# Layer 0's scan: one product moved from GpSimd to Vector, edges read in place, norm weight and bias fused, a new pace for the planner

## The chip, the cores and the metric

The kernel runs on one core of a Trainium2 chip. A core has TensorE (PE, with weight loads PEld), VectorE (DVE), ScalarE (ACT), GpSimd (POOL) and SyncE (SP), each with its own queue of instructions that it works off in order, and 16 DMA engines. The metric is device time in microseconds. Engines wait for each other through semaphores.

## The reference

The input is x of 4 samples, 96 channels and 128 x 128 pixels. Four layers follow each other, each as x = x + layer(norm(x)). Layer 0 is the one that the change touches; of it, with L = 128 * 128:

```
xz = einsum('oc,bchw->bohw', in_proj_w, x); xc, z = split(xz)
u = silu(depthwise_conv3x3(xc) + conv_b)              # (B, C, L)
xs = stack([u, u reversed])                           # two directions k
dts, Bs, Cs = split(einsum('bkcl,kdc->bkdl', xs, x_proj_w))
delta = softplus(einsum('bkrl,kcr->bkcl', dts, dt_proj_w) + dt_proj_b)
h_l = exp(delta_l * A) * h_(l-1) + delta_l * xs_l * B_l        # the scan over L
y_l = h_l * C_l;  ys = y + D * xs
y = ys[forward] + reversed ys[backward]
y = (y - mean_c) * rsqrt(var_c + 1e-5) * out_norm_w + out_norm_b
out = scale_w * (out_proj_w @ (y * silu(z)))
```

Layer 1 has small convolutions and Fourier transforms of two thirds of the channels. Layer 2 is a deformable convolution: a convolution gives each pixel nine offsets, and at each the four neighbouring pixels are gathered and weighed. Layer 3 transforms the image by a DCT, runs a scan with 16 states over four quadrants, and transforms back.

## The kernel before, in words

Each sample goes through three pieces. The *front* is layer 0, layer 1 and the offsets of layer 2; its results go to DRAM (`x1`, `x2`, `quad_d` with the pixels laid out for gathering, `idx_d`, `w4_d`). The *back* is layer 2's gathering, layer 3's head (`layer3_head`) and its first transform. Then comes layer 3's scan (`layer3`), with nothing beside it.

The main loop puts the back of one sample beside the front of the next one. In time this gives: the front of sample 0 alone (the *head stretch*); three *beside-stretches*, in which a back and a front run together (in the second and third the inverse transform of the sample before also runs beside the front's first block), each followed by layer 3's scan; a last stretch with a back and no front; the last scan and the last inverse.

**Gathering.** One gather (`indirect_dma_start`, tile `l2_g`, shown as `l_g`) is issued by Pool and fetches 128 pixels with four neighbours of 96 channels; there are 128 rows x 9 taps = 1152 gathers a sample. Beside a front there is room for four rows (`rows` = 4 from `back`), so that the gathers of a row wait until the row four before has been weighed. `weigh` multiplies the four neighbours by their weights: for each gather two instructions on Scalar and two on Vector (`l_sm`, `l_part`), and sums over several taps on Vector. PE then transposes and multiplies.

**Layer 0's scan** is the pool `l0b` with its function `scan(k, n)`. Each of the two directions k has 32 chunks of 512 columns, 64 in all, and the generators are staggered so that the directions alternate. For one chunk PE makes `pd`; Scalar makes softplus in three steps (`tmp`, and `dl` by Relu), Vector adds them (`dl + tmp`); PE makes `pB`; Scalar makes `dA = exp(dl * A)`; Vector multiplies `du = uc * pB` and Pool multiplies `du = du * dl`; Vector's `tensor_tensor_scan` makes `h`, starting from the edge of the chunk before in the same direction, which Scalar copies into a tile of its own (`l0_e`); PE makes `pC`, and Vector multiplies `h` by it in place. In the first half of the chunks the product goes to DRAM (`part_d`). In the second half the other direction's product is read back, and a tail follows: PE adds up and centres (`pm`), Scalar squares and copies (`sq`, `ct`), PE makes the variance (`pv`), Scalar makes its inverse root by Ln and Exp, Vector multiplies (`ct * sq`), Scalar applies the norm's weight and bias (Identity), Vector multiplies by `sz`, PE projects (`po`), Vector adds x and takes statistics.

**The order** is made by a planner (`Program`). All instructions of back (lane 0) and front (lane 1) are recorded, not issued. Each lane is first planned alone (`measure`): every instruction gets a start by the costs in `cost` and the times at which its inputs and buffers are ready. These starts become due times: distances between starts are multiplied by the `pace` that was set when the instruction was recorded, and the whole is scaled to 0..1. Then `issue` merges the lanes: among the instructions that can start within 0.17 us of the earliest on that engine, the one with the smallest due time is next. So a lower pace makes a part of the front fall due in less of the back's time. `self.program.pace` is 0.1 over layer 0's scan and 1.0 elsewhere. A DMA's cost is a pair: what the issuing engine is held for, and its landing, for which the model's single DMA resource is held; its data are ready 2.0 us behind that. The merged order is then fixed in each engine's queue. An instruction is issued through a helper, so nearly all of the profile's rows carry line L65 (SP's DMAs L412) and are told apart by their tiles.

Of the kernel before, what the change touches and what calls it, by code (L numbers as in the profile page):

```python
# [22 lines left out]
F32 = mybir.dt.float32  # L23
F32R = mybir.dt.float32r
I32 = mybir.dt.int32
AF = mybir.ActivationFunctionType
ALU = mybir.AluOpType
# [4 lines left out]
C, H, W = 96, 128, 128  # L32
L = H * W
CH = 512
# [202 lines left out]
class Program:  # L237
# [121 lines left out]
    def cost(self, engine, name, out, ins):  # L359

        if engine == "SP":
            v = next(v for v in [out, *ins] if isinstance(v, View) and v.tile.kind == "SBUF")
            return 0.35, 1.4e-5 * v.at[0].size * (v.rows[1] - v.rows[0])
        n = max(out.at[0].size, ins[0].at[0].size if name == "bn_stats" else 0)
        if name == "indirect_dma_start":
            return 1.25, 0.3
        if engine == "PE":
            if name == "transpose":
                return 1.1 * 0.00085 * n, None
            m = out.rows[1] - out.rows[0]  # L370
            share = (0.25 if m <= 32 else 0.5 if m <= 64 else 1.0) if n > 256 else 1.0
            return 1.1 * share * max(0.165, 0.005 + 0.001667 * n), None
        if engine == "ACT":
            return (0.055 + 0.0008 * n if name == "copy" else 0.19 + 0.00079 * n), None
        if engine == "POOL":
            return 0.2 + 0.002 * n, None
        if name == "tensor_tensor_scan":
            return 0.1 + 0.00214 * n, None
        fast = name in ("tensor_copy", "tensor_scalar", "memset") and all(
            v.tile.kind == "SBUF" for v in [out, *ins]  # L380
        )
        late = 0.12 if name == "scalar_tensor_tensor" and n > 200 else 0.0
        return (0.135 if n < 200 else 0.105) + late + n / (1800 if fast else 1024), None
# [128 lines left out]
class Net:  # L512
# [132 lines left out]
    def layer0(self, xin, T, beside):  # L645
        nc, a = self.nc, self.a
        u_d, sz_d, part_d = self.plane("u_d"), self.plane("sz_d"), self.plane("part_d")
        st0, T.st1 = self.stats_tile(), self.stats_tile()
        with self.program.pool(name="l0w", bufs=1) as wp, self.program.pool(name="l0p", bufs=1, space=PSUM) as ps:
# [71 lines left out]
                yield from staggered(jobs + ([beside(ps, wt)] if beside else []), 1)  # L721


            self.program.pace = 0.1
            with self.program.pool(name="l0b", bufs=3) as wb:
                edges = [None, None]

                def scan(k, n):
                    t = n if k == 0 else NCH - 1 - n
                    s = slice(t * CH, (t + 1) * CH)  # L730
                    uc = wb.tile([C, CH], F32, name="l0_uc", tag="uc", bufs=6)
                    nc.sync.dma_start(out=uc, in_=u_d[:, s])
                    second = n >= NCH // 2
                    if second:
                        xc = wb.tile([C, CH], F32, name="l0_x", tag="x", bufs=4)
                        nc.sync.dma_start(out=xc, in_=xin[:, s])
                        sz = wb.tile([C, CH], F32, name="l0_z", tag="z", bufs=4)
                        nc.sync.dma_start(out=sz, in_=sz_d[:, s])
                    yield
                    yield  # L740
                    pd = ps.tile([C, CH], F32, name="l0_pd", tag="b", bufs=1)
                    nc.tensor.matmul(out=pd, lhsT=wd[:, k, :], rhs=uc, start=True, stop=True)
                    yield
                    dl = wb.tile([C, CH], F32, name="l0_dl", tag="dl")
                    tmp = wb.tile([C, CH], F32, name="l0_tmp", tag="tmp")
                    bias = v[:, 1 + k : 2 + k]
                    nc.scalar.activation(tmp, pd, AF.Abs, bias=bias, scale=1.0)
                    nc.scalar.activation(dl, pd, AF.Relu, bias=bias, scale=1.0)
                    nc.scalar.activation(tmp, tmp, AF.Exp, scale=-1.0)
                    nc.scalar.activation(tmp, tmp, AF.Ln, bias=1.0, scale=1.0)  # L750
                    nc.vector.tensor_tensor(dl, dl, tmp, ALU.add)
                    pB = ps.tile([C, CH], F32, name="l0_pB", tag="c", bufs=2)
                    nc.tensor.matmul(out=pB, lhsT=wbc[:, 2 * k, :], rhs=uc, start=True, stop=True)
                    yield
                    dA = wb.tile([C, CH], F32, name="l0_dA", tag="dA")
                    nc.scalar.activation(dA, dl, AF.Exp, scale=negA[:, k : k + 1])
                    du = wb.tile([C, CH], F32, name="l0_du", tag="du")
                    nc.vector.tensor_tensor(du, uc, pB, ALU.mult)
                    yield
                    nc.gpsimd.tensor_tensor(du, du, dl, ALU.mult)  # L760
                    yield
                    h = wb.tile([C, CH], F32, name="l0_h", tag="h", bufs=5)
                    prev = edges[k]
                    if k == 0:
                        nc.vector.tensor_tensor_scan(
                            h, dA, du, 0.0 if prev is None else prev, ALU.mult, ALU.add
                        )
                        edge = h[:, CH - 1 : CH]
                    else:
                        nc.vector.tensor_tensor_scan(  # L770
                            h[:, ::-1], dA[:, ::-1], du[:, ::-1],
                            0.0 if prev is None else prev, ALU.mult, ALU.add,
                        )
                        edge = h[:, 0:1]
                    edges[k] = wb.tile([C, 1], F32, name="l0_e", tag="edge", bufs=6)
                    nc.scalar.copy(edges[k], edge)
                    if second:
                        part = self.load(wb, part_d[:, s], [C, CH], "l0_part", 3)
                    pC = ps.tile([C, CH], F32, name="l0_pC", tag="c", bufs=2)
                    nc.tensor.matmul(out=pC, lhsT=wbc[:, 2 * k + 1, :], rhs=uc, start=True, stop=True)  # L780
                    yield
                    nc.vector.tensor_tensor(h, h, pC, ALU.mult)
                    if not second:
                        nc.sync.dma_start(out=part_d[:, s], in_=h)
                        yield
                        return
                    yield


                    pm = ps.tile([C, CH], F32, name="l0_pm", tag="a", bufs=2)  # L790
                    nc.tensor.matmul(out=pm, lhsT=center[:, 1, :], rhs=uc, start=True, stop=False)
                    nc.tensor.matmul(out=pm, lhsT=center[:, 0, :], rhs=part, start=False, stop=False)
                    nc.tensor.matmul(out=pm, lhsT=center[:, 0, :], rhs=h, start=False, stop=True)
                    yield
                    ct = wb.tile([C, CH], F32, name="l0_ct", tag="ct")
                    sq = wb.tile([C, CH], F32, name="cn_s", tag="sq")
                    nc.scalar.activation(sq, pm, AF.Square)
                    nc.scalar.copy(ct, pm)
                    yield
                    pv = ps.tile([C, CH], F32, name="cn_v", tag="a", bufs=2)  # L800
                    nc.tensor.matmul(out=pv, lhsT=self.cavg, rhs=sq, start=True, stop=True)
                    yield
                    nc.scalar.activation(sq, pv, AF.Ln, bias=self.eps[:C], scale=1.0)
                    nc.scalar.activation(sq, sq, AF.Exp, scale=-0.5)
                    yield
                    nc.vector.tensor_tensor(ct, ct, sq, ALU.mult)
                    yield
                    nc.scalar.activation(ct, ct, AF.Identity, bias=v[:, 8:9], scale=v[:, 7:8])
                    yield
                    nc.vector.tensor_tensor(ct, ct, sz, ALU.mult)  # L810
                    yield
                    po = ps.tile([C, CH], F32, name="l0_po", tag="a", bufs=2)
                    nc.tensor.matmul(out=po, lhsT=woT, rhs=ct, start=True, stop=True)
                    yield
                    nc.vector.scalar_tensor_tensor(xc, po, v[:, 9:10], xc, ALU.mult, ALU.add)
                    nc.vector.bn_stats(T.st1[:, t, :], xc)
                    nc.sync.dma_start(out=T.x1[:, s], in_=xc)
                    yield

                yield from staggered((scan(k, n) for n in range(NCH) for k in range(2)), 2)  # L820

    def layer1(self, T):
# [1562 lines left out]
```

## Time and profile before

| what | us |
|---|---|
| time before, median of 3 (15122.8 to 15134.95) | 15123.15 |
| the profiled execution's own time | 15123.18 |
| its span | 15121.3 |
| PE, DVE, ACT, POOL busy | 12434.4, 11294.8, 8958.7, 10394.8 |

Where the stretches lie, by the first and last start of their instructions in the trace (us from the span's start):

| stretch | layer 0's scan (`pd` first, last) | gathers first, last | transform's last copy (`l_xo`) |
|---|---|---|---|
| head | 263.8, 590.9 | none | none |
| beside 1 | 1727.5, 2149.6 | 1304.1, 3163.9 | 3375.9 |
| beside 2 | 5354.6, 5764.3 | 4836.4, 6720.4 | 6933.9 |
| beside 3 | 8913.8, 9325.3 | 8397.4, 10277.7 | 10488.5 |
| last (no front) | none | 11949.5, 13413.1 | 13591.4 |

The scan's end lies some 30 to 40 us behind its last `pd`. In the second beside-stretch the front's pieces start at: statistics 4848, convolution 4943, scan 5355, layer 1's transforms 5876 (their last product 6211), layer 1's convolution 6248, offsets 6551 (last 6906).

How to read the profile: a group's row gives the line, engine, operation, output and input tiles, forms and count; then busy us and the mean ns of one; then the idle time just before them and what ended it. A row of windows gives, for each engine, busy us and in brackets the number of instructions, then the clock that PE was granted, the DMA engines' share and GB/s. Each fp32 product of PE appears as two records, so 128 records of `pd` are 64 products.

### The profile page before, as it was taken

What the parts mean: (1) busy time and instruction counts of PE and PEld (TensorE: products, weight loads), DVE (VectorE), ACT (ScalarE), POOL (GpSimd) and SP (SyncE); (2) the same over time, 40 slices, a digit from 0 to 9 for tenths busy, and PEclk for the clock granted to TensorE, in tenths of its full rate; (3) what the DMA queues carried; (4) which work ended last, traced back from release to release, by engine and by line L of the source; (5) the groups of instructions that cost most, each with busy time, mean ns of one, the idle gap of its engine ahead of it and who ended that gap; (6) DMA issues with size and microseconds to landing.
All of it is one profiled execution on the core that took longest, in us unless ns stands there. A gap on an engine that the chain in (4) does not pass through costs nothing. (4 is left out here: it accounts for less than half of the span.)

```text
span 15121.3 us, 175326 instructions
## 1 busy us (share of the span) xinstructions
PE 12434.4 (82%) x48096; PEld 5808.6 (38%) x48096; DVE 11294.8 (75%) x21519; ACT 8958.7 (59%) x21605; POOL 10394.8 (69%) x7936
## 2 busy tenths in 40 slices
PE   7897887879997978888999688888999744459998
PEld 3353334343332334444333233534333422233334
DVE  3626686668998587677999578666999765548997
ACT  3614685556664576555666467555666465546664
POOL 2104747748998765765999674773999877748997
PEclk9997898989998989989999899998999855579999
DMA  4546659766666767876666765976666755556666
GB/s 115 143 127 201 191 167 253 229 201 183 187 197 193 234 181 213 239 218 185 194 189 194 218 208 167 259 227 192 194 188 194 216 171 165 167 149 181 189 197 192
DMA packets 1326732, 2914.81 MB, mean 193 GB/s; under 512 B 282864, under 2 KB 768944, under 8 KB 1211440
## 3 DMA queue, kind: packets, MB, share of 16 engines
q1 hardware_dynamic: 1027376, 1997.21, 45.8%
q0 software_dynamic: 298368, 906.38, 20.2%
q8 instruction: 382, 6.26, 0.2%
q14 instruction: 606, 4.96, 0.1%
HBM read 2455.28 MB, written 447.48 MB: 192 GB/s over the span
## 5 line engine op out<-in xcount | busy, mean ns | idle before, releaser
L65 POOL DMA_INDIRECT l_g<-quad_d,l_i x4608 | 4648.1, 1009 | 2541.0 <-issue 1319.5
L65 POOL TENSOR_TENSOR l_hc<-l_h,l_cl 128x1024 f32<-128x1024 f32 x1536 | 3609.7, 2362 | 287.9 <-DVE l_h L65 259.0
L65 PE MATMUL l_py<-l_hc,ident 128*128 128x512 f32 x6144 | 3068.4, 610 | 185.9 <-POOL l_hc L65 182.4
L65 DVE TENSOR_TENSOR_SCAN l_h<-l_dA,l_carry,l_dB 128x512 f32<-128x512 f32 x2304 | 2863.6, 1266 | 1.7
L65 DVE SCALAR_TENSOR_TENSOR l_sm<-l_g,l_v,l_sm 128x96 f32<-128x96 f32 x4608 | 1491.3, 324 | 1137.8 <-ACT l_sm L65 1041.2
L65 ACT ACTIVATE l_dA<-l_dl,l_al 128x512 f32<-128x512 f32 x2304 | 1637.4, 718 | 1111.6 <-DVE l_h L65 1102.3
L65 ACT ACTIVATE l_sm<-l_g,l_v 128x96 f32<-128x96 f32 x4608 | 1677.6, 369 | 731.2 <-DMA l_g<-quad_d,l_i 634.4
L65 ACT ACTIVATE l_part<-l_g,l_v 128x96 f32<-128x96 f32 x4608 | 1654.8, 363 | 234.9 <-DVE l_sm L65 234.4
L65 PEld LDWEIGHTS l_py<-l_hc,ident 128*128 128x128 f32 x6144 | 1133.6, 192 | 1352.9 <-issue 829.2
L65 PE MATMUL l_pc<-l_sT,l_wk 128*96 128x256 f32 (+1 forms) x3584 | 1244.2, 471 | 418.8 <-ACT l_sT L65 418.1
L65 PE MATMUL l_pt<-ident,l_sm 128*128 128x128 f32 (+1 forms) x3584 | 798.3, 327 | 909.4 <-DVE l_sm L65 827.9
L65 DVE TENSOR_TENSOR l_dB<-l_du,l_pB 128x512 f32<-128x512 f32 x2304 | 1493.9, 678 | 49.5 <-POOL l_du L65 26.7
L65 DVE SCALAR_TENSOR_TENSOR l_part<-l_g,l_v,l_part 128x96 f32<-128x96 f32 x4608 | 1485.8, 323 | 36.3 <-ACT l_part L65 35.6
L65 PE MATMUL l_pB<-l_bc,pick 128*128 128x512 f32 x2304 | 1399.8, 635 | 135.4 <-DVE l_dB L65 121.5
L65 POOL TENSOR_TENSOR l_dP<-l_du,l_cl 128x512 f32<-128x512 f32 x768 | 978.6, 1274 | 101.0 <-DMA l_cl<-bc_d 74.6
L65 PEld LDWEIGHTS l_pt<-ident,l_sm 128*128 128x128 f32 (+1 forms) x3584 | 522.9, 165 | 1317.5 <-DVE l_sm L65 922.1
L65 DVE TENSOR_TENSOR_SCAN l_h<-l_dQ,l_carry,l_dP 128x512 f32<-128x512 f32 x768 | 971.8, 1265 | 58.3 <-POOL l_dP L65 54.9
L65 PEld LDWEIGHTS l_pc<-l_sT,l_wk 128*96 128x96 f32 (+1 forms) x3584 | 646.5, 200 | 944.3 <-ACT l_sT L65 513.2
L65 PE MATMUL l_pc<-rows,l_wc 96*32 96x508 f32 (+3 forms) x6912 | 919.6, 601 | 2.4 <-DVE rows L65 2.4
L65 POOL TENSOR_TENSOR l_du<-l_du,l_dl 96x512 f32<-96x512 f32 x256 | 339.6, 1327 | 834.1 <-DVE l_dl L65 487.1
L65 ACT COPY l_sT<-l_pt 128x512 f32<-128x512 f32 (+1 forms) x1024 | 520.8, 522 | 656.1 <-PE l_pt L65 654.0
L65 PE MATMUL l_p<-rows,l_c 96*32 96x508 f32 (+3 forms) x6912 | 823.1, 598 | 83.9 <-issue 46.7
(265 smaller groups left out, 19771.8 us busy)
## 6 DMA issues: line engine op xcount, KB each, us to landing
l_cl<-bc_d SPq DMA_DIRECT2D x512, 1280.0 KB
l_cl<-bc_d SPq DMA_DIRECT2D x512, 640.0 KB
quad_d<-l_qt SPq DMA_DIRECT2D x124, 768.0 KB
l_g<-quad_d,l_i POOLq DMA_INDIRECT x4608
x<-l_x SPq DMA_DIRECT2D x352, 192.0 KB
l_uc<-u_d SPq DMA_DIRECT2D x256, 192.0 KB
l_x<-x SPq DMA_DIRECT2D x224, 192.0 KB
l_xs<-x SPq DMA_DIRECT2D x116, 256.0 KB
```

What stands on the lines that cost most here:

```text
L65: ins = op(*args, **kw).ins
```

## The change

1. `du = du * dl` is issued on Vector, no longer on Pool.
2. The edge is no copy: the next scan of the same direction reads the last (or first) column of `h` itself. For that the product with `pC` no longer overwrites `h`, but goes to a new tile `y` (three buffers); `h` has four buffers in place of five, `tmp` two in place of three.
3. The norm's weight is applied by the copy of `pm` to `ct` (activation Copy with a scale), the bias together with the product by `sz` in one `scalar_tensor_tensor` on Vector; the Identity step on Scalar goes.
4. The planner: the pace over the scan is 0.3 in place of 0.1, and a gather's landing 0.66 in place of 0.3.

```diff
         if name == "indirect_dma_start":
-            return 1.25, 0.3
+            return 1.25, 0.66
...
-            self.program.pace = 0.1
+            self.program.pace = .3
...
-                    tmp = wb.tile([C, CH], F32, name="l0_tmp", tag="tmp")
+                    tmp = wb.tile([C, CH], F32, name="l0_tmp", tag="tmp", bufs=2)
...
-                    nc.gpsimd.tensor_tensor(du, du, dl, ALU.mult)
-                    yield
-                    h = wb.tile([C, CH], F32, name="l0_h", tag="h", bufs=5)
+                    nc.vector.tensor_tensor(du, du, dl, ALU.mult)
+                    yield
+                    h = wb.tile([C, CH], F32, name="l0_h", tag="h", bufs=4)
...
-                        edge = h[:, CH - 1 : CH]
+                        edges[k] = h[:, CH - 1 : CH]
...
-                        edge = h[:, 0:1]
-                    edges[k] = wb.tile([C, 1], F32, name="l0_e", tag="edge", bufs=6)
-                    nc.scalar.copy(edges[k], edge)
+                        edges[k] = h[:, 0:1]
...
-                    nc.vector.tensor_tensor(h, h, pC, ALU.mult)
+                    y = wb.tile([C, CH], F32, name="l0_y", tag="y")
+                    nc.vector.tensor_tensor(y, h, pC, ALU.mult)
                     if not second:
-                        nc.sync.dma_start(out=part_d[:, s], in_=h)
+                        nc.sync.dma_start(out=part_d[:, s], in_=y)
...
-                    nc.tensor.matmul(out=pm, lhsT=center[:, 0, :], rhs=h, start=False, stop=True)
+                    nc.tensor.matmul(out=pm, lhsT=center[:, 0, :], rhs=y, start=False, stop=True)
...
-                    nc.scalar.copy(ct, pm)
+                    nc.scalar.activation(ct, pm, AF.Copy, scale=v[:, 7:8])
...
-                    nc.scalar.activation(ct, ct, AF.Identity, bias=v[:, 8:9], scale=v[:, 7:8])
-                    yield
-                    nc.vector.tensor_tensor(ct, ct, sz, ALU.mult)
+                    nc.vector.scalar_tensor_tensor(ct, ct, v[:, 8:9], sz, ALU.add, ALU.mult)
```

## The prediction

> **What bounds the kernel now.** I read the page's groups first, then windows of 60 us over one beside-stretch (the second, 4836 to 6934 us), then groups and waits inside its scan, then the same for the head stretch, where the front runs alone.
>
> The page, groups of Pool:
>
> ```profile
> L65 POOL DMA_INDIRECT l_g<-quad_d,l_i x4608 | 4648.1, 1009 | 2541.0 <-issue 1319.5
> L65 POOL TENSOR_TENSOR l_du<-l_du,l_dl 96x512 f32<-96x512 f32 x256 | 339.6, 1327 | 834.1 <-DVE l_dl L65 487.1
> ```
>
> A gather holds Pool for 1009 ns and then 286 ns of issue (1319.5 / 4608). The 256 products du*dl, 64 to a scan, are the other thing on that queue, and Pool stands idle before them for 834 us in all. Windows of 60 us in the second beside-stretch: two in the scan, two behind it.
>
> ```profile
> 5400.00:5460.00 60.00, 47.08 (x103) 15.99 (x101) 59.49 (x82) 48.75 (x111) 44.22 (x33) 0.91 0.52 152
> 5640.00:5700.00 60.00, 57.22 (x143) 22.14 (x142) 49.85 (x79) 52.02 (x103) 20.97 (x17) 1.00 0.50 156
> ...
> 6300.00:6360.00 60.00, 60.00 (x458) 21.14 (x455) 36.93 (x118) 31.52 (x111) 45.61 (x48) 1.00 0.79 234
> 6600.00:6660.00 60.00, 44.17 (x175) 29.38 (x175) 53.13 (x174) 44.08 (x150) 46.28 (x46) 0.72 0.81 260
> ```
>
> Columns: PE, PEld, Vector, Scalar, Pool, then clock, DMA share, GB/s. Behind the scan Pool makes 46 to 48 gathers in 60 us, one per 1.27 us, the rate of the last gather stretch where nothing of the front runs (1152 gathers in 1464 us). So outside the scan the gathers set the pace, whatever the other engines do. In the scan Vector is full (59.5 of 60) in the first half and PE nearly so in the second, and Pool makes only 17 to 33 instructions. Groups of Vector over the scan (5390 to 5830), then the same for the head stretch (262 to 575) and for the gathers' own work behind the scan (5880 to 6240):
>
> ```profile
> L65 DVE TENSOR_TENSOR_SCAN l_h<-l_dA,l_e,l_du 96x512 f32<-96x512 f32 x62 | 78.8, 1272 | 5.7 <-POOL l_du L65 5.7
> L65 DVE TENSOR_TENSOR l_dl<-l_dl,l_tmp 96x512 f32<-96x512 f32 x61 | 54.7, 897 | 2.3 <-ACT l_tmp L65 1.9
> L65 DVE SCALAR_TENSOR_TENSOR l_part<-l_g,l_v,l_part 128x96 f32<-128x96 f32 x112 | 49.2, 446 | 0.1
> L65 DVE SCALAR_TENSOR_TENSOR l_sm<-l_g,l_v,l_sm 128x96 f32<-128x96 f32 x113 | 47.9, 431 | 1.4 <-ACT l_sm L65 1.4
> L65 DVE TENSOR_TENSOR l_ct<-l_ct,cn_s 96x512 f32<-96x512 f32 x32 | 21.6, 674 | 7.3 <-ACT cn_s L65 7.3
> ```
>
> Head stretch:
>
> ```profile
> L65 DVE TENSOR_TENSOR l_dl<-l_dl,l_tmp 96x512 f32<-96x512 f32 x61 | 51.3, 841 | 10.8 <-ACT l_tmp L65 8.0
> ```
>
> Behind the scan:
>
> ```profile
> L65 DVE SCALAR_TENSOR_TENSOR l_sm<-l_g,l_v,l_sm 128x96 f32<-128x96 f32 x265 | 82.7, 312 | 36.5 <-ACT l_sm L65 34.4 <-DMA l_g<-quad_d,l_i 1.5
> ```
>
> The reader is to see that one form costs 674 ns (ct*cn_s, two SBUF inputs) and 897 (dl) in the same scan, and that the gathers' weighing costs 431 to 446 ns there and 312 behind it. dl is as slow (841) in the head stretch, where there are no gathers. What stands beside the slow ones in both is Pool's product. Waits of the scan (5354 to 5800):
>
> ```profile
> POOL l_du L65 <- DVE l_dl L65: 110.5, 18, 16.2
> DVE l_h L65 <- POOL l_du L65: 5.7, 5, 1.8
> DVE l_ct L65 <- ACT l_ct L65: 5.0, 7, 0.9
> ```
>
> Behind each of those 18 waits of Pool, gathers stand in its queue.
>
> **The change, part by part.** The profiled execution's own time is 15123.18 us (span 15121.3), the median 15123.15; the sum is made against 15123.2.
>
> *A scan beside gathers, the same gathers in it (three of them).* Vector's own work in a scan of 64 chunks, 32 of them with a tail, by the rows of the second stretch: scans 81.3, dl 64 x 0.897 = 57.4, du 42.4, h*pC 43.1, ct*cn_s and ct*z 21.6 each, x 23.7, statistics 22.1: 313 us. Added: 64 products with two SBUF inputs, at ct*cn_s's 0.674: +43. Removed with Pool's product: the excess of dl, 64 x (0.897 - 0.674) = -14. ct*z becomes a three-operand instruction, 0.740 as x's row: +2. Weighing returns to 0.312: 225 x 0.312 against 97.1: -27. The waits of l_h for Pool and of l_ct for Scalar's weight and bias go: -11. Sum -7. Bounds: nothing is relieved and the product runs at 0.897, +59; all of Vector's idle time in the scan (34 of 440 us) goes as well, -30. I take -7, since the head stretch and the windows behind the scan are two rows that clear the gathers and leave Pool's product.
>
> *Off Scalar:* 64 edge copies and 32 Identity steps. Scalar is busy for 49 to 53 of 60 us, so nothing, as long as Vector or PE is full; covered by them. *tmp at two buffers, h at four, y at three (the store to part_d frees it):* a chunk of the first half takes about 5 us beside gathers, three chunks 15; I take nothing, at most 5 us a scan. *The edge in place* lets a scan wait for Vector's own earlier scan of the same direction in place of Scalar's copy; the scan of the other direction and several instructions lie between, and Scalar, behind whose queue that copy stood, is no longer asked: nothing.
>
> *More gathers in the scan.* By the order in which the program's instructions stand, between the first and the last pd product there were 126, 119 and 119 gathers and are now 154, 149 and 149: about 30 more. Each costs Vector two weighings of 0.312 and a ninth of two sums (0.664 + 0.560): 0.76 us, so +23 to the scan. Outside they are missing: (1884 - 446) / (1152 - 119) = 1.39 us each there, so -42; at Pool's 1.27 it would be -38.
>
> *The rest of the gathers moves too,* because the pace and the larger landing alter due times: layer 1's transforms get 325 instead of 279 gathers, the offsets 36 instead of 126. In gather-bound stages that is a shift and no gain. But of the offsets' 96 matmuls 69 instead of 48 (60 instead of 36 in the first stretch) now stand behind the last gather, beside layer 3's head and its transform. From last gather to last copy of the transform:
>
> ```profile
> L65 POOL DMA_INDIRECT l_g<-quad_d,l_i x1152: 940/946/2428, 4836.4 to 6720.4; - x192
> ...
> L65 DVE COPY l_xo<-t_p x24: 680/692/694, 6870.1 to 6933.9; 128x512 f32<-128x512 f32 x24
> ```
>
> 213 us with 48 matmuls of the offsets; 212 with 36 (first stretch), 178 with none (last). From 36 to 48 nothing, from 0 to 36 34 us: 21 more cost between 0 and 20; I take +8.
>
> *The landing of 0.66 us* is what the page shows for a gather (20.2% of 15121 us over 4608). In the transforms' stretch 5880 to 6240 266 gathers take 360 us, 22 more than at 1.27. A better order can take between none and all of it; I take a third, -7.
>
> Per beside-stretch: -7 + 23 - 42 + 8 - 7 = -25; three: -75.
>
> *The head stretch* has no gathers, and its 20 us windows show two limits:
>
> ```profile
> 340.00:360.00 20.00, 15.32 (x33) 4.65 (x31) 18.62 (x22) 16.44 (x32) 6.57 (x6) 1.00 0.37 108
> ...
> 500.00:520.00 20.00, 20.00 (x48) 7.59 (x47) 16.82 (x24) 17.30 (x33) 3.32 (x3) 1.00 0.47 148
> ```
>
> In the first half Vector sets the pace: per chunk +0.674 and -0.167 for dl: 32 x 0.507 = +16. In the second PE does: 48 records in 20 us are three chunks of eight products, 6.67 us each; Vector after the change has 0.674 + 0.665 + 0.674 + 1.274 + 0.674 + 0.684 + 0.741 + 0.741 + 0.691 = 6.82, 0.15 over: +5. Sum +21 (10 to 40).
>
> Total -75 + 21 = -54: **15,069 us, -0.36%**.
>
> *A rule against the change.* The two-input product now locks against the gathers. The row: in this scan a gather takes 1172 ns, its median over the whole trace is 946. The Trainium skill, "GPSIMD Engine Reference", section Specifications, says that GpSimd's SBUF interfaces are shared with VectorE and that instructions with two SBUF inputs contend, which the new product is and the one that stays on Vector (dl) too. By the row nothing is added, as Pool stands idle for over 200 of 446 us of the scan; by the rule, if every gather of the scan grew by another 226 ns, 149 would take 34 us more of Pool, still inside that idle time.
>
> **Rivals.**
> 1. *Vector, already full, gets 43 us and no relief* (slower). If the slow dl and weighing come from the gathers' own writes, the product runs at 0.897 and the weighing stays: 59 + 29 - 42 + 8 = +54 a stretch, and +42 in the head stretch: 15,327. With half of the relief 15,200. For it: 59.49 of 60. Against: 841 without gathers. It decides from 18 us a stretch, that is weighing above 0.37 us in the scan.
> 2. *The offsets' tail gives it back* (no change): +20 there, gathers at 1.27, no help from the landing: -7 + 23 - 38 + 20 = -2 a stretch; 15,138. For it: 93 us of Pool's waits in that tail are for Vector. Against: 36 and 48 matmuls cost the same.
> 3. *The order was what held the gathers back* (more gain). If the rate outside the scan goes from 1.39 to 1.33, 1003 gathers give another 60 us a stretch: about 14,900; with half of it 14,980. For it: windows of 38 to 41 gathers between those of 47. Against: much of that is the step from scan to transforms, a chain that stays.
>
> **How the numbers follow.** The forecast has 0.45 (its own range 15,010 to 15,115), rival 1 0.26, rival 2 0.14, rival 3 0.15. A measurement of this kernel tells about 0.2% (30 us) from no change. Faster by more: 0.40 of the forecast's and rival 3, 0.55. Within: 0.05 of the forecast and most of rival 2, 0.17. Slower: 0.28. The range leaves out the far halves of rivals 1 and 3: 14,960 to 15,205.
>
> **What would show it.** Right: dl and the product near 0.68 us on Vector, weighing near 0.32 in the scan; the three scans within 10 to 25 us of 446 with some 150 gathers; first to last gather 1855 to 1870 us instead of 1884; the head stretch 15 to 30 us longer; the tails 213 to 225. Wrong: weighing still above 0.4 in the scan, gathers at less than 44 per 60 us in layer 1's transforms (their DMA share is up to 1.05 already), or Vector waiting for y's buffers.

## The result and the profile after

The changed kernel takes 15,222.8 us (median of 4 runs, 15,210.08 to 15,248.54) against 15,123.47 us for the kernel before (4 runs): a ratio of 1.0069, 95% interval 1.0054 to 1.0084. It is slower by 0.7%, where the prediction had it 0.36% faster, and it lies beyond the upper end of the range. The profiled execution after took 15,210.08 us (span 15,208.3), 87 us more than that of before.

Where the stretches lie after, and before in brackets, by first and last starts in the two traces (us):

| | beside 1 | beside 2 | beside 3 |
|---|---|---|---|
| layer 0's scan, first to last `pd` | 419 (422) | 407 (410) | 407 (412) |
| layer 1's transforms, first `sp_a` to last `sp_c` | 453 (402) | 466 (394) | 466 (391) |
| layer 1's convolution, first to last `l_p` | 381 (269) | 354 (271) | 354 (271) |
| first to last gather | 1876 (1860) | 1882 (1884) | 1886 (1880) |
| tail: last gather to last `l_xo` | 234 (212) | 242 (213.5) | 241 (211) |
| first gather to last `l_xo` | 2110 (2072) | 2124 (2098) | 2126 (2091) |
| gathers between first and last `pd`, in program order | 154 (126) | 149 (119) | 149 (119) |

The head stretch did not change: the first gather starts at 1302.8 us, where it started at 1304.1. Each beside-stretch is 27 to 38 us longer, 100 us in all, of which the rest gives back 13 (the two profiled spans differ by 87). So the question is in the beside-stretches: the scan holds 30 more gathers and is no longer for it, and still first to last gather took no less time.

The page of after, groups of Pool and of PE, and the page of before, the same PE group:

```profile
L65 POOL DMA_INDIRECT l_g<-quad_d,l_i x4608 | 4647.3, 1009 | 3730.5 <-issue 1282.3
...
L65 PE MATMUL l_p<-rows,l_c 96*32 96x508 f32 (+3 forms) x6912 | 1076.4, 599 | 30.3 <-DMA rows<-cat_d 20.5
```

```profile
L65 PE MATMUL l_p<-rows,l_c 96*32 96x508 f32 (+3 forms) x6912 | 823.1, 598 | 83.9 <-issue 46.7
```

The gather itself is as before, 1009 ns. Pool stood idle before its gathers for 3730.5 us (2541.0 before), but that says little: before, Pool also stood idle for 834.1 us ahead of its products and worked on them for 339.6, and with the products gone both count as idle time ahead of gathers. What is new is in PE's row: the products of layer 1's convolution (`l_p`, 96x32 on PE) hold PE for 253 us more, though there are as many of them (6912 records) and each takes as long (599 against 598 ns). Busy time counts overlapping records once, so the same products lie less beside each other than they did. That group's 253 us are about the growth of the convolution in the table: 112 + 83 + 83 = 278.

Windows of 60 us in the second beside-stretch of after: two in the scan, and two in layer 1's convolution (PE, PEld, Vector, Scalar, Pool, then clock, DMA share, GB/s):

```profile
5400.00:5460.00 60.00, 42.27 (x101) 15.64 (x100) 59.24 (x126) 54.82 (x136) 32.43 (x30) 0.87 0.55 166
5640.00:5700.00 60.00, 58.20 (x142) 21.54 (x141) 58.85 (x106) 47.81 (x87) 15.87 (x14) 1.00 0.58 173
6420.00:6480.00 60.00, 60.00 (x342) 16.71 (x338) 29.52 (x93) 23.16 (x79) 34.17 (x35) 1.00 0.59 171
6600.00:6660.00 60.00, 60.00 (x338) 17.11 (x334) 30.51 (x97) 24.24 (x82) 36.09 (x37) 1.00 0.56 163
```

In the scan Vector works off 126 and 106 instructions in 60 us (82 and 79 before, in the same windows). Behind it the sight is new: PE is full at the full clock, makes only some 340 records where before it made 458 in such a window, and Pool makes 35 to 37 gathers where it made 48. Vector, Scalar and Pool are all half idle. PE sets the pace there.

Vector's groups in the scan of after (5390 to 5830):

```profile
L65 DVE TENSOR_TENSOR_SCAN l_h<-l_dA,l_h,l_du 96x512 f32<-96x512 f32 x62 | 79.1, 1277 | 3.9
L65 DVE SCALAR_TENSOR_TENSOR l_sm<-l_g,l_v,l_sm 128x96 f32<-128x96 f32 x170 | 52.2, 307 | 0.0
L65 DVE SCALAR_TENSOR_TENSOR l_part<-l_g,l_v,l_part 128x96 f32<-128x96 f32 x170 | 52.2, 307 | 0.0
...
L65 DVE TENSOR_TENSOR l_du<-l_du,l_dl 96x512 f32<-96x512 f32 x62 | 42.1, 679 | 0.8
L65 DVE TENSOR_TENSOR l_dl<-l_dl,l_tmp 96x512 f32<-96x512 f32 x62 | 41.9, 676 | 0.0
```

The relief came as forecast: `dl` fell from 897 to 676 ns, weighing from 431 and 446 to 307 ns, the new product costs 679 ns, and these five groups wait for less than 5 us in all. Pool's longest waits over this scan (5372 to 5815; total us, times, longest):

```profile
POOL l_g L65 <- ACT l_dl L65: 114.8, 3, 69.8
POOL l_g L65 <- ACT l_tmp L65: 51.0, 4, 25.4
```

The 110.5 us in which Pool waited with a product for `dl` are gone, and Pool now waits about as long with a gather. A gather that needs the place of the row four before it waits for that row's weighing, and the weighing stands in Scalar's and Vector's queues among the scan's instructions, as the planner placed it. So the wait was moved, not removed; for which weighing each of these waits was is read from the order of the queues and was not traced.

### The profile page after: what moved, and what is told of

It is laid out like the page before. It is cut to its first block, busy times and chain, and to the rows that moved or that the text cites. A ratio compares the mean times of both kernels' runs of the same rounds, so it can differ in the third digit from the quotient of the medians.

```text
span 15208.3 us, 174389 instructions
## 1 busy us (share of the span) xinstructions
PE 12672.2 (83%) x48096; PEld 5786.6 (38%) x48096; DVE 11304.5 (74%) x21775; ACT 8869.1 (58%) x21225; POOL 10055.2 (66%) x7680
## 5 line engine op out<-in xcount | busy, mean ns | idle before, releaser
L65 POOL DMA_INDIRECT l_g<-quad_d,l_i x4608 | 4647.3, 1009 | 3730.5 <-issue 1282.3
L65 DVE SCALAR_TENSOR_TENSOR l_sm<-l_g,l_v,l_sm 128x96 f32<-128x96 f32 x4608 | 1428.2, 313 | 1196.1 <-ACT l_sm L65 1158.9
L65 ACT ACTIVATE l_sm<-l_g,l_v 128x96 f32<-128x96 f32 x4608 | 1632.9, 369 | 840.7 <-DMA l_g<-quad_d,l_i 692.0
L65 ACT ACTIVATE l_part<-l_g,l_v 128x96 f32<-128x96 f32 x4608 | 1617.2, 364 | 332.3 <-DVE l_sm L65 327.0
L65 DVE SCALAR_TENSOR_TENSOR l_part<-l_g,l_v,l_part 128x96 f32<-128x96 f32 x4608 | 1436.6, 315 | 112.3 <-ACT l_part L65 109.6
L65 PE MATMUL l_p<-rows,l_c 96*32 96x508 f32 (+3 forms) x6912 | 1076.4, 599 | 30.3 <-DMA rows<-cat_d 20.5
L65 PE MATMUL l_pc<-rows,l_wc 96*32 96x508 f32 (+3 forms) x6912 | 955.6, 597 | 2.4 <-DVE rows L65 2.4
L65 PEld LDWEIGHTS l_pB<-l_bc,pick 128*128 128x128 f32 x2304 | 436.5, 190 | 1058.0 <-DVE l_dB L65 834.8
```

The costliest lines, as they stand in the source:

```text
L65: ins = op(*args, **kw).ins
```

## The experiments

Two theories after the first look. *Theory O (order):* the new order, made by the new landing or the new pace, puts other work between the 32-column products of layer 1's convolution, and this is the loss; the code of the scan is a gain. *Theory V (code):* the new code in itself costs more than it brings, through Vector or the buffers, and the order only follows it.

What the order looks like. Layer 1's convolution issues its 32-column products in sets of four, each of a set for another group of 32 columns; a stretch has 864 of them, 216 sets. PE by time, before and then after (start us, busy us of a run of like instructions, count of records; one product is two records):

```profile
6359.26 3.60 PE L65 MATMUL l_p<-rows,l_c 96*32 96x508 f32 x32
6362.80 0.76 PE L65 MATMUL l_pt<-ident,l_sm 128*128 128x128 f32 x5
6363.49 1.91 PE L65 MATMUL l_p<-rows,l_c 96*32 96x508 f32 x14
```

```profile
6401.02 1.05 PE L65 MATMUL l_p<-rows,l_c 96*32 96x512 f32 x2
6402.00 0.44 PE L65 MATMUL l_pt<-ident,l_sm 128*128 128x128 f32 x2
6402.37 1.05 PE L65 MATMUL l_p<-rows,l_c 96*32 96x512 f32 x2
6403.34 0.44 PE L65 MATMUL l_pt<-ident,l_sm 128*128 128x128 f32 x2
6403.71 2.76 PE L65 MATMUL l_p<-rows,l_c 96*32 96x512 f32 x22
```

Before, 32 records (four sets) take 3.60 us, 0.90 us a set. After, transposes of gathered rows (`l_pt`) stand between single products, and a single product holds PE for 1.05 us, longer than a whole set holds it in a row of sets. Counted in program order, there are 37, 42 and 42 places before, in the three stretches, at which other work of PE stands between two products of one set, and 127, 112 and 112 after. Such a place is called a *break* here. They fall into 37, 39 and 39 sets before and 70, 66 and 66 after; where the expectations below speak of so many broken sets, their numbers are breaks.

The runs below are comparisons with a kernel before that ran on the same chip beside them. All of them compute the whole result.

**The new code with the old numbers of the planner (e1_code_only).** The changed kernel with two lines put back:

```diff
-            return 1.25, 0.66
+            return 1.25, 0.3
...
-            self.program.pace = .3
+            self.program.pace = 0.1
```

> The new scan (product on Vector, edges in place, norm weight and bias fused) with the planner as before (pace 0.1, landing 0.3). Theory A, broken sets: the time was lost in layer 1's convolution, where the new order puts transposes of the gathered rows between the four 32-column products that otherwise run side by side; here the order breaks as few sets as before (37, 42 and 42 of 216 in the three stretches), so the convolution keeps its 271 us per stretch, the scans get some 25 us shorter each, and the kernel is faster than before: 15,040 to 15,080. Rival B, Vector: the product on a full Vector is what cost the time; then this is slower than before, 15,160 to 15,210, and the scans are longer than 410 us from first to last pd.

Measured: 15,024.07 us, ratio 0.9939 (0.9922 to 0.9955), 92 us less than the kernel before beside it (15,115.61) and 16 below the range expected. Scans 388, 374, 376 us with 126, 110 and 110 gathers in them, transforms 414, 403, 401, convolution 268, 270, 270 us, 37 breaks in each stretch (the second and third have five fewer than expected). Theory V falls: the code alone is a gain of 0.6%. Vector in the scan of that run (5327 to 5735):

```profile
L65 DVE TENSOR_TENSOR l_dl<-l_dl,l_tmp 96x512 f32<-96x512 f32 x64 | 43.4, 678 | 1.6 <-ACT l_tmp L65 1.6
```

**The larger landing alone (e2_landing_only).** The kernel before with

```diff
-            return 1.25, 0.3
+            return 1.25, 0.66
```

> The kernel before with a gather's landing of 0.66 and nothing else changed. Theory A: this number alone makes the order that breaks the sets (78, 129 and 129 of 216 broken), so layer 1's convolution takes 330 to 360 us in place of 271 in the second and third stretch, l_p's busy time rises from 823 to some 1050 us, and the kernel takes 15,220 to 15,330. Rival B: 15,110 to 15,150, no change, as the product is still on GpSimd. Theory C, the tail: only the offsets' matmuls behind the last gather (60 of 96 in place of 48) count: tails 25 to 30 us longer and the sum 15,190 to 15,215, with the convolution at 271.

Measured: 15,317.81 us, ratio 1.0133 (1.0116 to 1.0150), 202 us more. No instruction of the scan differs from before, only the order. Breaks 78, 129 and 129; convolution 318, 379 and 380 us; transforms 449, 447 and 451. The page:

```profile
L65 PE MATMUL l_p<-rows,l_c 96*32 96x508 f32 (+3 forms) x6912 | 1047.1, 597 | 50.3 <-DMA rows<-cat_d 37.8
```

This one number of the planner's model is worth more than the whole loss.

**The larger pace alone (e3_pace_only).** The kernel before with

```diff
-            self.program.pace = 0.1
+            self.program.pace = .3
```

> The kernel before with pace 0.3 over layer 0's scan and nothing else changed: some 40 more gathers in each scan, as few broken sets as before (34 to 40), 48 and 60 of the offsets' matmuls behind the last gather in place of 36 and 48. Theory A: layer 1's convolution stays at 271 us, and the kernel within 40 us of before, 15,090 to 15,165. Theory C, the tail: tails 25 us longer, 15,180 to 15,210. Rival D, gathers in the scan: Pool's products and waits make the scan 30 us longer, 15,190 to 15,240.

Measured: 14,973.96 us, ratio 0.9906 (0.9890 to 0.9923), 142 us less; better than any of the three theories had it. The scan holds 171, 161 and 161 gathers and grows to 444, 427 and 427 us; first to last gather falls to 1810, 1818 and 1822; breaks 34, 40 and 40, convolution as before. So it is the landing that breaks the sets, not the pace.

**After, with the sets kept whole (e4_after_sets_whole).** The changed kernel with one rule more for the planner: once the first product of a set is issued, PE gets nothing else before the set is complete. It holds for layer 0's convolution too, whose products are of the same kind.

```diff
+        if op.engine == "PE" and name == "matmul" and out.rows[1] - out.rows[0] <= 32 and out.at[0].size > 256:
+            op.set = self.sets // 4
+            self.sets += 1
...
+            if op.engine == "PE":
+                rest = [e for e in starts if e[-1].engine == "PE" and e[-1].set is not None and e[-1].set == self.open_set]
+                if rest:
+                    start, *_, op = rest[0]
+                self.open_set = op.set
```

> The changed kernel with a rule in the planner that a set of four 32-column products, once begun, is finished before PE gets anything else. Pace 0.3, landing 0.66 and the new scan stay. Theory A: l_p's busy time falls from 1076 to some 750 to 820 us, the convolution from 354 to 270 to 290 us per stretch, where the gathers (233 at 1.27) set the pace; 60 to 80 us less per stretch: 14,980 to 15,040. Theory C or rival B: the convolution gets shorter but the gathers and the tail keep the end, within 40 us of 15,210.

Measured: 14,930.14 us, ratio 0.9877 (0.9861 to 0.9894) to the kernel before. That is 293 us under the changed kernel's 15,222.8 (from the two medians, on different chips), by a rule that touches nothing but the order, and better than the 14,980 to 15,040 expected. Layer 1's convolution takes 268, 262 and 261 us, which is 113, 92 and 93 less, 298 in all; layer 0's, first to last product, takes 6, 9 and 17 less. The page, the window in the convolution, and PE by time:

```profile
L65 PE MATMUL l_p<-rows,l_c 96*32 96x508 f32 (+3 forms) x6912 | 795.8, 598 | 23.7 <-DMA rows<-cat_d 16.7
```

```profile
6300.00:6360.00 60.00, 60.00 (x462) 20.51 (x455) 37.33 (x115) 32.07 (x108) 46.00 (x47) 1.00 0.79 232
```

```profile
6327.92 1.06 PE L65 MATMUL l_p<-rows,l_c 96*32 96x508 f32 x8
```

A set of four that stands alone between other work takes 1.06 us (8 records), a lone product 1.05 us: with the set split in two, the same products cost twice as much. With the sets whole PE is back at 462 records in 60 us and Pool at 47 gathers.

**Is it the rule that gains, or the landing's order that loses?** The rule alone on the kernel before (e6 and e10), and the landing with the rule (e12). Beside them the product alone (e5 and e9), and the new scan with landing 0.3, the rule and other paces (e7, e8, e11, e13). The chips of e5 to e11 take 16,667 and 16,775 us for the kernel before, so those seven are read by ratios and by comparisons inside their own group (e5 to e8 and e9 to e11). With nothing of the front running, Pool makes 209 gathers in 300 us there (e6), where before makes 238.

The rule alone is the block above on the kernel before:

> The kernel before with sets of four 32-column products kept whole, nothing else. If broken sets only cost where they are many, the 42 and 48 broken sets of each stretch are worth about 1 us of PE each, mostly hidden behind the gathers' 1.27 us: 15,090 to 15,120. If PE's time counts everywhere in the two convolutions, 80 us a stretch or more come off, as with e4: below 14,950, and e4's gain says nothing of the landing.

> e6 once more on such a chip. Few broken sets hidden behind the gathers: 15,080 to 15,120, against 15,115; PE's time counting everywhere: below 15,000.

Measured: ratios 1.0016 (0.9993 to 1.0039) and 0.9997 (0.9982 to 1.0012), no difference on these two chips. This doesn't carry over to the others. In layer 1's convolution of e10 PE is busy for 335 to 345 us of 382 to 388, with a granted clock of 0.89 in the window below, and Pool makes some 32 gathers in 60 us:

```profile
7200.00:7260.00 60.00, 50.73 (x330) 17.57 (x327) 28.42 (x90) 23.41 (x80) 31.65 (x32) 0.89 0.58 166
```

In the convolutions of before PE is busy throughout, 269 to 271 us. The rule alone was not run on such a chip, so whether it is a gain of its own there is open; in e13 below, with whole sets and as few runs, the convolutions take 257, 255 and 255 us, 13 to 16 less than before, but more than the rule is changed in it.

Landing and rule together on the kernel before, against e2 the rule alone is added:

> The kernel before with landing 0.66 alone, as e2, but with sets of four 32-column products kept whole; the gathers stand at the same places of the front as in e2 (495 by the end of the second scan, 819 by the end of the transforms, 1062 by the end of the convolution). Theory A, all of the landing's loss is broken sets: l_p's busy time back from 1047 to some 800 us in all, and the ratio to before 0.99 to 1.00 in place of e2's 1.013. Rival, the gathers' new places cost by themselves: a ratio of 1.005 or more with the sets whole.

Measured: 15,089.19 us beside 15,135.05, ratio 0.9970 (0.9958 to 0.9981); e2 without the rule had 1.0133. By the ends of the second stretch's scan, transforms and convolution 495, 819 and 1062 gathers stand in the program order, as in e2; 119 of them are in the scan, 117 in e2. The page:

```profile
L65 PE MATMUL l_p<-rows,l_c 96*32 96x508 f32 (+3 forms) x6912 | 798.3, 597 | 50.1 <-DMA rows<-cat_d 38.0
```

So with the sets whole the loss of 1.3% is gone: it was the price of the breaks. What is left, 0.3%, is a gain of landing and rule together. Against the kernel before, divided by the breaks that were added, the price is much the same in four cases:

| | convolution longer by, us | breaks more | us per break |
|---|---|---|---|
| after, stretch 1 | 112 | 90 | 1.24 |
| after, stretches 2 and 3 | 83 | 70 | 1.19 |
| landing only, stretch 1 | 49 | 41 | 1.20 |
| landing only, stretches 2 and 3 | 108 | 87 | 1.24 |

That is not what every break costs. In before, after, e2 and e4 alike a run of one to four of these products takes 1.04 to 1.06 us, one of five to eight 1.9, of nine to twelve 2.76, of thirteen to sixteen 3.6. So a break costs most where it leaves single products and pairs (102 single ones in the first stretch of after, none in that of before), and little where it cuts long runs, as in before. An estimate of 0.2 us for each run and 0.86 us for each started four of products gives 209 us of PE for the first stretch before and 307 after; the traces have 210 and 308.

**The product alone (e5, e9).** The kernel before with

```diff
-                    nc.gpsimd.tensor_tensor(du, du, dl, ALU.mult)
+                    nc.vector.tensor_tensor(du, du, dl, ALU.mult)
```

> The kernel before with the product du*dl on Vector and nothing else: edges copied by Scalar, weight and bias apart, planner as before, and nearly the order of before. Relief theory: the scan's gain in e1 (374 us from first to last pd in place of 410) comes from taking Pool's product from beside Vector; dl falls from 897 to near 680 ns, the weighing from 435 to near 312, the scan to 375 to 388 us and the kernel to 15,025 to 15,060. Rival: the gain came from the edges and the fused norm; then the scan is 405 us or longer and the kernel 15,100 to 15,180, as 43 us were added to a full Vector in each scan.

> e5 once more, on a chip with the gathers at 1.27 us. e5's scans were 30 to 40 us shorter than those of e6, where the product is still on Pool. Relief theory: scans of 375 to 388 us in place of 410, and 15,025 to 15,070 against 15,115. If the slower gathers of e5's chip hid a loss, or if the edges and the fused norm made e1's gain, 15,090 to 15,180.

Measured: ratios 0.9960 (0.9944 to 0.9976) and 0.9969 (0.9955 to 0.9984), in the part of the relief theory. The scans take 397, 381 and 389 us in e5 and 400, 381 and 380 in e9, where e6 and e10, with the product on Pool, have 439, 419, 419 and 438, 422, 421. Vector in the second scan of e9 (5960 to 6340) and of e10 (5940 to 6340):

```profile
L65 DVE SCALAR_TENSOR_TENSOR l_sm<-l_g,l_v,l_sm 128x96 f32<-128x96 f32 x132 | 40.4, 308 | 10.9 <-ACT l_sm L65 7.2 <-ACT t_t L65 3.0 <-issue 0.5
...
L65 DVE TENSOR_TENSOR l_dl<-l_dl,l_tmp 96x512 f32<-96x512 f32 x58 | 39.5, 681 | 0.2 <-issue 0.2
```

```profile
L65 DVE TENSOR_TENSOR l_dl<-l_dl,l_tmp 96x512 f32<-96x512 f32 x58 | 55.0, 950 | 3.3 <-ACT l_tmp L65 3.2
L65 DVE SCALAR_TENSOR_TENSOR l_sm<-l_g,l_v,l_sm 128x96 f32<-128x96 f32 x127 | 52.5, 416 | 14.3 <-ACT l_sm L65 12.4 <-DMA l_g<-quad_d,l_i 0.8 <-ACT l_tmp L65 0.7
```

With the product moved (e10 has the rule besides, which acts on the products of the two convolutions), `dl` costs 681 in place of 950 ns and weighing 308 in place of 416, with as many gathers beside them. What slowed Vector was Pool's product, not the gathers. The trace of before shows how, on Vector and on Pool:

```profile
5430.95 0.67 DVE L65 TENSOR_TENSOR l_h<-l_h,l_pC 96x512 f32<-96x512 f32 x1
5431.55 1.51 DVE L65 TENSOR_TENSOR l_dl<-l_dl,l_tmp 96x512 f32<-96x512 f32 x1
```

```profile
5431.22 1.28 POOL L65 TENSOR_TENSOR l_du<-l_du,l_dl 96x512 f32<-96x512 f32 x1
```

`dl` begins while Pool's product runs and ends 0.56 us behind it; each of the 17 `dl` of that scan that begin so ends 0.55 to 0.57 us behind Pool's product. In that scan (5354 to 5800) 18 of the 64 `dl` overlap a product of Pool and take 1.41 us on average; the other 46 take 0.68, also those beside a gather. Of the weighings `l_sm`, 22 overlap one and take 1.15 us, the other 103 take 0.31. The 41 products `h * pC` that overlap one, with one input in PSUM, take 0.675 us, as the others do. So 897 and 431 ns are means of a few long instructions and many of the usual length. The Trainium skill, "SBUF — State Buffer", section Who interferes with whom, says that a VectorE instruction with two SBUF inputs contends with a GpSimd instruction that reads SBUF and not with one that only writes there; the rows on Pool's product agree with it.

Scans shorter by 30 to 42 us are about what e1 gained with all of the new code (34 and 35), which leaves little for the edges, the fused weight and bias and the buffers.

**The best pace for the new scan (e7, e8, e11, e13).** The changed kernel with the rule, landing 0.3, and pace 0.2 (e7) or 0.4 (e8, e11, e13):

```diff
-            return 1.25, 0.66
+            return 1.25, 0.3
...
-            self.program.pace = .3
+            self.program.pace = .4
```

> The new scan, landing 0.3, pace 0.2 and sets kept whole. If the gains of the scan (92 us in e1) and of the pace (142 us in e3 at 0.3, here half of it) add up, 14,900 to 14,965; if they are the same time won twice, 14,965 to 15,020. Against e4 (14,930) it tells whether the larger landing is worth anything once the sets are whole.

> The same with pace 0.4: 45 more gathers in the scan than before and 60 to 63 of the offsets' matmuls behind the last gather. If the gathers outside still set the pace, 14,840 to 14,920; if the scan, where Vector is full, pays for them and the tail grows by 15 us a stretch, no better than pace 0.2, 14,920 to 14,990.

> e8 once more on such a chip: new scan, pace 0.4, landing 0.3, sets whole. Gains add up: 14,840 to 14,920. Scan and tail pay for the moved gathers: 14,920 to 14,990, no better than e4.

> The new scan, pace 0.4, landing 0.3, sets whole, as e8 and e11. On a chip with gathers at 1.27 us: gains add up, 14,840 to 14,920; scan and tail pay for the moved gathers, 14,920 to 14,990. On a chip with slower gathers a ratio to before of 0.985 to 0.99, as in e8 and e11.

Measured: pace 0.2 0.9889 (0.9866 to 0.9912); pace 0.4 0.9865 (0.9839 to 0.9892), 0.9890 (0.9860 to 0.9920), and e13 14,893.3 us beside 15,135.05, 0.9840 (0.9823 to 0.9856). On the scale of 15,115 us the run at 0.2 and two of three at 0.4 lie where the gains were to add up, e11 where scan and tail were to pay. Between the two paces, 16,488.18 and 16,436.46 us on one chip, the intervals overlap, though each run of e8 is below each of e7. e13 is the best version: 181, 164 and 164 gathers stand in scans of 445, 410 and 409 us, and first to last gather takes 1794, 1783 and 1774. It is 1.6% faster than the kernel before, and so beats the changed kernel as well, which has 1.0069.

What stays open: by which step of the planner a larger landing leads to single products between transposes. The order shows that it does, the runs of products show what it costs; why was not traced. The rule alone on a chip of the first kind, the new code with the changed pace and the old landing, without the rule, and the new way of reading edges with the product left on Pool were not run.

## Why the prediction was wrong

**The failed step** is the term for the landing, "A better order can take between none and all of it; I take a third, -7", and the premise on which it and the -42 stand, "outside the scan the gathers set the pace, whatever the other engines do". The landing alone costs 202 us (e2, about 67 a stretch), and it does so in layer 1's convolution, where PE sets the pace. Its range ran from nothing to a gain of 22; a loss was not in it. With the sets whole, landing and rule together gain 46 us (e12, 15 a stretch); how much of that is the landing's is not shown.

The premise could have been seen to fail in the window that the prediction itself shows: 6300 to 6360 has PE at 60.00 of 60 us beside Pool's 48 gathers. Two engines were at their limit there, and only one was spoken of. Nor were 46 to 48 gathers the rate of all that stands behind the scan: the six windows from 5880 to 6240 have 40 to 47. The program order could be had as well: only gathers and offsets' products were counted in it. The convolution's products stand there in 53, 57 and 57 unbroken runs before and 173, 152 and 152 after, of which 102, 78 and 78 are a single product (0, 4 and 4 before). The trace of before has the price of a single product as well, from one of the four:

```profile
6279.05 1.04 PE L65 MATMUL l_p<-rows,l_c 96*32 96x508 f32 x2
```

By it 95 to 120 more runs cost between nothing and 99 to 125 us a stretch, an estimate from the order and this row; the convolution grew by 83 and 112. The upper end is five times the -25 of the sum, so that with this in it the sign was open.

**The scan beside the same gathers: -7, measured -34** (e1's first stretch, with 126 gathers as before; -35 in the two others, which have nine fewer). The instructions' durations were right: `dl` 676 to 681 ns (0.674 taken), the product 679 (0.674), weighing 307 to 309 (0.312), `ct*z` 747 (0.740). What was mis-sized is mainly Vector's idle time. Between first and last `pd` of the first stretch it falls from 38 to 15 us, where 11 less was taken, and busy time from 384 to 374, where the sum has 4 more. I took only the waits that were named as Pool's and Scalar's; the lower bound, -30, with all idle time gone, is nearer, and is passed by 4.

**30 more gathers in it: +23.** After has 39 more gathers in each of the second and third scans than e1, and these are 33 and 31 us longer: 0.82 us each, where 0.76 was taken. This step held, as far as two different orders can be compared.

**The gathers missing outside: -42 at 1.39 us each.** By the same quotient, the time outside the scan over the gathers there, the second stretch has 1.39 in e1, 1.37 in e3 (pace alone), 1.35 in e4, and 1.44 after: (1882 - 443) / (1152 - 149). 0.045 us more for each of 1003 gathers is 45 us. First to last gather was to fall by 33 us a stretch (-7 + 23 - 42 - 7; the signs listed at its end say 14 to 29); it rose by 7 on average, and fell by 72 once the sets were whole.

**The tail: +8, measured +22, +29 and +30**, over the upper bound of 20. In e4, with nearly as many matmuls of the offsets behind the last gather (60, 66 and 66; 60, 69 and 69 after), it is +15, +12.5 and +16. So about half of it goes with the offsets' work, as said, and the other half came and went with the order of PE; which work of the tail that was is not settled.

**The head stretch: +21, measured -1.** The added products found room. Windows of 100 us of its scan, before and after:

```profile
300.00:400.00 100.00, 76.56 (x166) 24.34 (x165) 90.93 (x107) 82.14 (x158) 33.39 (x27) 1.00 0.37 109
```

```profile
300.00:400.00 100.00, 81.39 (x176) 26.43 (x177) 99.97 (x140) 81.31 (x141) 0.00 (x0) 1.00 0.37 109
```

Vector goes from 107 to 140 instructions in that time and from 90.93 to 99.97 us, and PE gets further, 176 records in place of 166. Vector had been called the limit at 18.62 of 20 us, but it had 9 of 100 us left, which went as in the scans beside gathers, and `dl` is now 679 ns where it was 841. Vector's groups over that scan (262 to 575):

```profile
L65 DVE TENSOR_TENSOR l_dl<-l_dl,l_tmp 96x512 f32<-96x512 f32 x61 | 41.4, 679 | 1.6 <-ACT l_tmp L65 1.4
```

**The rule against the change** was set at nothing, and rightly: a gather in the second scan of after takes 1110 ns (172 of them), where it took 1172. Vector's two-input product on the new engine did not lengthen the gathers beside it.

**The rivals.** Rival 1 (no relief) is refuted by 307 ns of weighing. Rival 2 (the tail gives it back) has its mechanism in the tails, but in e4, where the sets are whole, they take back some 15 of 72 us a stretch. Rival 3 (the order held the gathers back) shows in e4, where 1.35 us a gather outside the scan is two thirds of its way to 1.33. The pace alone (e3) is more the forecast's own trade: 42 gathers more in each of the later scans, which grow by 17 and 15 us, and 83 and 74 us less outside, of which 42 at 1.39 are 58. The mechanism that decided is none of the three. The sign that was named for being wrong, fewer than 44 gathers in 60 us in the transforms, could not tell: from 5880 to 6240 after has 41 to 48, four windows of six below 44, and before has 40 to 47, two below. The loss lay behind them, in the convolution, with 35 and 37 where before had 48.

**The sum.** Per beside-stretch: scan -3 where +16 was forecast, first to last gather outside it +10 where -49, tail +27 where +8; +33 where -25, the average of +38, +27 and +35. With the sets whole (e4) a stretch takes 58 us less than before: the breaks, which stand in the sum at nothing, cost 91, and all the rest gained 58 where the sum has 25. The gains are real and do not add: e1, e3 and e12 gained 92, 142 and 46 us, and e4, which has all three, 185.

## What to carry to other kernels

A constant in a scheduler's model is an edit to every queue: read what moved on each engine, and not only around the instruction whose cost was changed; here one number for a DMA's landing, alone, cost 1.3% through the order of matmuls. Where small matmuls run beside each other in different columns of the array, treat the set as one unit of the order: one of them alone takes as long as four, and no row's mean duration shows it, only the group's busy time. And when a window shows two engines at their limit, price the change for both.

## What was not expected of the hardware

A single 32-column product (96 rows, 508 to 512 columns of data) holds PE for 1.05 us, a set of four that stands alone for 1.06, and four sets in a row for 0.90 us each; a transpose of 128x128 on each side of a single product undoes that. The Trainium skill, "TensorEngine Tiling (Array Packing)", section Key Properties, says that different tiles of the array can run matmuls in parallel and that changing the tiling mode drains TensorE. The first agrees with 1.06 us for four. Whether a drain is part of the loss the traces do not separate: a run of one to four takes 1.04 to 1.06 us in before, after and e2, whatever stands on either side.

A two-input Vector instruction is held up while Pool's product runs, with the end of that product as its release: 18 of 64 `dl` overlap one and take 1.41 us in place of 0.68. Spread over the scan this is a mean of 220 to 270 ns (`dl` 897 or 950 ns against 676 to 681).
